# A graph attention layer on one core: x parts of more chunks ahead of the last stage, residuals further ahead, the shift split on ScalarE

## The chip, the core and the metric

The kernel runs on one core of a Trainium2 chip. The core has five engines, each with its own instruction queue: PE (TensorE, matrix products into PSUM), DVE (VectorE), ACT (ScalarE), POOL (GpSimd) and SP (SyncE, which here only issues DMAs). PSUM has eight banks of 128 partitions by 512 fp32 numbers. The metric is the device time of one execution in microseconds (us); lower is better.

## What is computed

12500 nodes with 128 features, 212500 edges sorted by target. In the reference, cut to what matters:

```python
Q, K, V = x @ WQ, x @ WK, x @ WV                    # 8 heads of 16
Eh = edge_attr @ WE
score = exp(clip(sum(K[src] * Q[dst] / 4 * Eh), -5, 5))
wV = segment_sum(V[src] * score, dst);  Z = segment_sum(score, dst)
h = x + wV / (Z + 1e-6)
h = (h - mean(h, nodes)) * rsqrt(var(h, nodes) + 1e-5) * bn_gamma + bn_beta
out = layernorm(x + h)                              # over the 128 features
```

The batch normalisation over nodes means that no output can be made before the last edge is done. With its factors a (scale) and b (offset) for each feature, the last stage computes layernorm(x + a*h + b) for each node.

## The kernel before, in words

Features lie on the 128 partitions: hx holds h transposed, 128 x 12500, and is updated in place. The edges are worked in groups g = 0 to NG-1 of up to eight tiles of 128 edges (L695 to L743). In each group POOL issues gathers of K and V rows, PE multiplies the edge features (`ehqe`, banks ps_e and ps_q), ACT and DVE form the products, PE turns them back (`turn_back`, L514, ps_t), DVE multiplies with K (`products`, L523), reduces to scores, ACT exponentiates, DVE forms the messages (L540), and PE sums them by target (`gather_sum`, L555 and L554, ps_a). ACT reads the sums out (L560), DVE divides (`denom`, `recip`, `attn`), PE turns the result and adds x (`add_x`, L580 and L581), ACT writes it into hx (`x_out`, L585), and DVE takes statistics (`bn_part`, L588). The order on each engine is written out by hand; each engine runs its list in that order and waits on semaphores.

After the groups come `norm_factors` (L357 to L362: the factors ab) and the last stage, `last_stage`, over 25 chunks of 512 nodes (the last has 212), taken in pairs: 0, 1, then (2,3), (4,5) to (22,23), and 24. For each chunk PE has to hold, in one bank, the centred sum x + a*h + b, nodes on partitions. `cent` is the matrix that subtracts the mean over features. There are two ways:

- A chunk in AHEAD: PE adds three products in the bank: the x part, `part_of_x` (L685, XR times cent, four matmuls), the h part (L820, hx times scaled_cent, four matmuls) and the shift b (L823 for chunk 0 in fp32, else L827, which multiplies bf16 pieces of the shift by ones). The x part doesn't need the factors, so `ahead(i)` can run it early, in the bank the chunk will use.
- Any other chunk: a residual y = a*h + x is made in SBUF, and PE centres it (L832, four matmuls). On POOL (odd chunks and 24) it takes two instructions (L799, L800) and includes b; on DVE (`on_vector`, even chunks from 8) one (L797), and PE adds the shift.

`split_shift` (L802 to L811) makes the shift: a small product into a bank, then five DVE instructions that split it into three bf16 rows. For each pair, ACT then squares one chunk whole (L847, DVE reduces it at L848) and the other in four pieces with accumulation (L852), takes the root (L854); DVE forms the reciprocal (L858) and the scaled output (L864), and SP stores it (L866). Banks are given out in the order of RING, chunk i taking entry i mod 8.

The order of the last stage is a software pipeline over the pairs:

```python
for i in range(len(pairs) + 4):
    for f, k in ((residual, i), (centred, i - 1), (variance, i - 1), (scaled, i - 2)):
```

so the residual of a pair stands one step ahead of its matmuls and squares. The residual buffers y are six. Before the change AHEAD is 0, 1, 2, 3, 4, 10 and 18; the x part of chunk 0 runs in the last group (L701), that of chunk 1 after add_x of the last group but one (L752), those of 2, 3 and 4 after the last add_x (L760), and those of 10 and 18 in the last stage itself.

Of the kernel before, what the change touches and what calls it, by code (L numbers as in the profile page):

```python
# [8 lines left out]
F32 = mybir.dt.float32  # L9
BF16 = mybir.dt.bfloat16  # L10
I32 = mybir.dt.int32
AF = mybir.ActivationFunctionType
# [4 lines left out]
P = 128  # L17
# [45 lines left out]
def gnn_kernel(  # L63
# [19 lines left out]
    nc = tc.nc  # L83
# [4 lines left out]
    NG = NW // 2  # L88
# [11 lines left out]
    psp = pps.enter_context(tc.tile_pool(name="psum", bufs=1, space=bass.MemoryType.PSUM))  # L100
# [105 lines left out]
    def issue(n=0):  # L206
        while len(queued) > n:
            f, *a = queued.pop(0)
            f(*a)

    def pace(step):
        if queued:
            f, *a = queued.pop(0)
            tc.add_manual_dep(f(*a).ins, step.ins.name,
                              mybir.DependencyInfo(mybir.DependencyClass.Sync, mybir.DependencyReason.DATA),
                              reason="pace")
# [13 lines left out]
    def fetch_rows(g, k, i):  # L230
        if i == 0:
            by_row[g] = rows.tile([P, 1, 2 * P], F32, name="byrow", bufs=2)
        _, ids = nc.values_load_multi_w_load_instructions(
            row_ids[i:i + 1, k * ROWS:(k + 1) * ROWS], engines=(ET.SP,), min_val=0, max_val=N - 1,
            skip_runtime_bounds_check_because="node ids")
        for p, r in enumerate(ids, i * ROWS):
            nc.sync.dma_start(by_row[g][p:p + 1, 0, :], kvd[ds(r, 1), :])
# [57 lines left out]
    def within(f, g):  # L295
        return f(g) if 0 <= g < NG else None
# [99 lines left out]
    B4 = 4 * P  # L396
# [4 lines left out]
    def width(i):  # L401
        return min(B4, N - i * B4)
# [172 lines left out]
    NEW = {}  # L575

    def add_x(g):
        NEW[g] = ps = (psp.tile([P, 4, P], F32, name="ps_e", bufs=2)[:, 0, :] if NG - 3 <= g < NG - 1 else
                       small_ps[:, 1, :])
        nc.tensor.matmul(ps, AT[g], ident, start=True, stop=False)  # L580
        return nc.tensor.matmul(ps, ident, XW[g], start=False, stop=True)  # L581
# [50 lines left out]
    for q in range(NQ):  # L632
# [3 lines left out]
        for g, a in piece.get(q, []):  # L636
            if a == 0:
                i = free.pop(0)
# [5 lines left out]
        k = q - first_step  # L644
# [28 lines left out]

    AHEAD = [0, 1, 2, 3, 4, 10, 18]
    RING = ["ps_q", "ps_q", "ps_t", "ps_t", "ps_e", "ps_e", "ps_a", "ps_m"]

    def blocks(i):
        n = width(i)  # L680
# [2 lines left out]
    def part_of_x(i, ps):  # L683
        for k, m in blocks(i):
            nc.tensor.matmul(ps[:m, k, :], XR[i][:, k * P:k * P + m], cent, start=(k == 0), stop=False)  # L685
# [3 lines left out]
    def ahead(i):  # L689
        if i in AHEAD:  # L690
            r = RING[i % len(RING)]
            PX[i] = psp.tile([P, 4, P], F32, name=r, bufs=RING.count(r))
            part_of_x(i, PX[i])

    for g in range(NG):  # L695
        within(load, g + 4)
        within(load_rel, g + 5)
        if g in fill:
            fetch_rows(*fill[g])
        within(products, g)  # L700
        if g == NG - 1:  # L701
            ahead(0)
        within(both_halves, g + 1)
        step = within(add_x, g - 3)
        step = within(q_mm, g + 3) or step
        if step is not None and queued:
            pace(step)
        issue()
        within(gather_sum, g - 1)
        if g + 1 < nxg and g + 1 not in SLOT:  # L710
            for _ in project_main(g + 1):
                pass
        within(turn_back, g + 1)
        within(scores, g)
        within(clip_exp, g)
        within(q_hi, g + 3)
        within(x_out, g - 3)
        within(sums_out, g - 1)
        within(q_lo, g + 2)
        within(denom, g - 2)  # L720
        within(recip, g - 2)
        within(attn, g - 2)
        within(q_window, g + 4)
        within(turned_onehot, g + 3)
        within(ehqe, g + 2)
        within(q_mid, g + 3)
        if g == NG - 1:
            add_x(g - 2)
        within(message, g)
        within(onehot, g + 1)  # L730
        if g == 2:
            load_last()
        for r in runs[1:]:
            if g == max(4, r[0] // 2 - 12):
                place(r)
        if g >= first_check and (g - first_check) % every == 0:
            check((g - first_check) // every)
        while free and todo and not pending:
            load_x()
        if g == NG - 2:  # L740
            flag = [nc.values_load(bad_i[0:1, 0:1], min_val=0, max_val=1 << 20,
                                   skip_runtime_bounds_check_because="a count")]
        bn_parts(2 * g - 5, 2 * g - 3)  # L743
# [5 lines left out]
    recip(last - 1)  # L749
    attn(last - 1)  # L750
    add_x(last - 1)
    ahead(1)  # L752
    sums_out(last)
    x_out(last - 1)
    denom(last)
# [1 line left out]
    attn(last)  # L757
    bn_parts(2 * last - 3, 2 * last + 1)
    add_x(last)
    for i in (2, 3, 4):  # L760
        ahead(i)
    x_out(last)
    for j in range(NCH):
# [6 lines left out]
    pairs = [[i] for i in range(min(2, NY))] + [list(range(i, min(i + 2, NY))) for i in range(2, NY - 1, 2)]  # L770
    if pairs[-1][-1] < NY - 1:
        pairs.append([NY - 1])
    if len(pairs[-1]) > 1 and width(NY - 1) < B4:
        pairs[-1:] = [[NY - 2], [NY - 1]]
    on_vector = {i for i in range(8, NY, 2) if width(i) == B4 and i not in AHEAD}
    by_reduce = {0, 2} | {i for i in range(3, NY, 2) if width(i) == B4}

    def last_stage(fin, bank, PX):
        Y, PY, V = {}, {}, {}
# [6 lines left out]
        shift = fin.tile([P, P], BF16, name="shift", bufs=1)  # L786
        scaled_cent = fin.tile([P, P], F32, name="scaled_cent", bufs=1)

        def residual(i):

            c, n = i * B4, width(i)
            if i in AHEAD:
                return
            Y[i] = fin.tile([P, B4], F32, name="y", bufs=6)
            y, h = Y[i][:, :n], hx[:, c:c + n]
            if i in on_vector:
                nc.vector.scalar_tensor_tensor(y, h, ab[:, 0:1], XR[i][:, :n], op0=OP.mult, op1=OP.add)  # L797
            else:
                nc.gpsimd.tensor_scalar(y, h, ab[:, 0:1], ab[:, 1:2], op0=OP.mult, op1=OP.add)  # L799
                nc.gpsimd.tensor_tensor(y, y, XR[i][:, :n], op=OP.add)  # L800

        def split_shift():  # L802
            ps = bank(6)[:65, 0, :]
            nc.tensor.matmul(ps, ab[:, 1:2].to_broadcast([P, 65]), cent, start=True, stop=True)
            rest = fin.tile([P, P], F32, name="rest", bufs=1)
            mid = fin.tile([P, P], BF16, name="mid", bufs=1)
            nc.vector.tensor_copy(shift[:65], ps)
            nc.vector.tensor_sub(rest[:65], ps, shift[:65])
            nc.vector.tensor_copy(mid[:65], rest[:65])
            nc.vector.tensor_copy(shift[32:33], mid[32:33])  # L810
            nc.vector.tensor_sub(shift[64:65], rest[64:65], mid[64:65])  # L811

        def centred(i):
            PY[i] = ps = PX[i] if i in PX else bank(i)
            c, full = i * B4, i in AHEAD
            if full:
                if i not in PX:
                    part_of_x(i, ps)
                for k, m in blocks(i):
                    nc.tensor.matmul(ps[:m, k, :], hx[:, c + k * P:c + k * P + m], scaled_cent, start=False,  # L820
                                     stop=False)
            if i == 0:
                nc.tensor.matmul(ps, ab[:, 1:2].to_broadcast([P, P]), cent[:, None, :].to_broadcast([P, 4, P]),  # L823
                                 start=False, stop=True)
                split_shift()
            elif full or i in on_vector:
                nc.tensor.matmul(ps, pick[:65], shift[:65, None, :].to_broadcast([65, 4, P]), start=not full,  # L827
                                 stop=full)
            if not full:
                whole = i in on_vector  # L830
                for k, m in blocks(i):
                    nc.tensor.matmul(ps[:m, k, :], Y[i][:, k * P:k * P + m], cent, start=not whole,  # L832
                                     stop=(k == 3 or not whole))
# [35 lines left out]
                    nc.sync.dma_start(out[c + k * P:c + k * P + m, :], o[:m, h, k, :])  # L869

        nc.vector.tensor_scalar(scaled_cent, cent, ab[:, 0:1], None, op0=OP.mult)
        for i in range(len(pairs) + 4):
            for f, k in ((residual, i), (centred, i - 1), (variance, i - 1), (scaled, i - 2)):
                if 0 <= k < len(pairs):
                    if f in (residual, centred):
                        for c in pairs[k]:
                            f(c)
                    else:
                        f(pairs[k])

    with tc.tile_pool(name="fin", bufs=3) as fin:
        last_stage(fin, lambda i: psp.tile([P, 4, P], F32, name=RING[i % 8], bufs=RING.count(RING[i % 8])), PX)
    pps.close()
# [140 lines left out]
```

## Time and profile before

| | |
|---|---|
| median of 3 runs | 2147.52 us (2146.24 to 2150.62) |
| the profiled execution | 2148.77 us, its span 2147.0 us |
| busy: PE, DVE, POOL, ACT | 1689.2, 1637.6, 1588.5, 626.3 us |
| last gathered sums of the last group (end of L555) | 2091.5 us |
| factors known (end of L362) | 2096.29 us |
| last DVE instruction ends | 2140.10 us |
| mean granted TensorE clock | 0.935 |

A busy PE includes waiting inside its pipeline, so its share isn't a distance from its peak. A timeline row gives start, duration, engine, line, operation, what is written and read with shapes, and in brackets the idle time before it and what ended it. An fp32 matmul shows as two rows of the PE count: "x8" is four matmuls. Line numbers are those of the kernel before; after the change lines from L702 on stand one to five lines lower.

### The profile page before, as it was taken

The numbers are of one execution on the slowest core, as the hardware profiler recorded it, in microseconds if no ns is written. First come the engines' busy times: TensorE is split into PE (matmuls) and PEld (weight loads), VectorE is DVE, ScalarE is ACT, GpSimd is POOL, SyncE is SP. The second block draws the span as 40 slices with busy tenths as digits, with TensorE's granted clock in tenths as the row PEclk, the third lists the DMA queues.
The fourth block names the chain that finished last, engine by engine and source line by source line (L and its number), as shares of the span: only waits on it lengthen the run. The fifth ranks groups of instructions, "written<-read, shape, count | busy, mean of one in ns | idle before, by whom it ended". The sixth has DMA issues, their size and how long they took to land. (4 is left out here: it accounts for less than half of the span.)

```text
span 2147.0 us, 36604 instructions
## 1 busy us (share of the span) xinstructions
PE 1689.2 (79%) x9398; PEld 1112.1 (52%) x9398; DVE 1637.6 (76%) x3574; ACT 626.3 (29%) x2472; POOL 1588.5 (74%) x1683
## 2 busy tenths in 40 slices
PE   8898888777777777777777877777777777777786
PEld 7565555444445454544555554545454445555455
DVE  4669999777877777777787777777777777777776
ACT  3343333232322222222222222222322222222225
POOL 7776777777777777777777777777777777777754
PEclk9999999999999999999999999999999999998988
DMA  9866666556555555555655555555655655655754
GB/s 302 277 189 183 180 201 190 176 169 178 170 179 168 173 173 167 178 172 167 180 167 175 174 170 177 167 179 157 182 180 168 180 168 155 193 168 155 228 169 122
DMA packets 179729, 386.77 MB, mean 180 GB/s; under 512 B 41838, under 2 KB 96151, under 8 KB 179511
## 3 DMA queue, kind: packets, MB, share of 16 engines
q0 software_dynamic: 78128, 212.05, 33.9%
q1 hardware_dynamic: 98038, 169.83, 25.6%
q10 hardware_dynamic: 3345, 2.48, 0.4%
q8 instruction: 77, 1.26, 0.2%
q14 instruction: 141, 1.16, 0.2%
HBM read 364.57 MB, written 19.63 MB: 179 GB/s over the span
## 5 line engine op out<-in xcount | busy, mean ns | idle before, releaser
L200 POOL DMA_INDIRECT slot<-kvd,srcs x1585 | 1502.2, 948 | 492.7 <-issue 430.6
L555 PE MATMUL ps_a<-msg,oh 128*128 128x136 f32 (+1 forms) x3322 | 573.9, 316 | 0.0
L523 DVE TENSOR_TENSOR p<-slot,ps_t 128x512 f32<-128x512 f32 (+1 forms) x408 | 272.0, 676 | 360.9 <-DMA slot<-kvd,srcs 336.2
L555 PEld LDWEIGHTS ps_a<-msg,oh 128*128 128x128 f32 (+1 forms) x3322 | 468.0, 185 | 86.4 <-issue 66.5
L535 ACT ACTIVATE ps_m<-s 128x64 f32<-128x64 f32 x208 | 47.3, 228 | 1328.0 <-DVE s L533 966.6
L493 PE MATMUL ps_e<-ea,w_e 128*128 128x512 f32 x832 | 409.0, 615 | 3.1 <-DMA ea<-eaT 2.8
L580 PE MATMUL ps_m<-ident,at 128*128 128x128 f32 x412 | 102.1, 332 | 304.6 <-DVE oh L457 299.5
L514 PE MATMUL ps_t<-ident,wt 128*128 128x128 f32 x1661 | 244.9, 286 | 104.7 <-DVE wt L506 103.5
L580 PEld LDWEIGHTS ps_m<-ident,at 128*128 128x128 f32 x412 | 66.2, 202 | 396.4 <-ACT q L483 353.5
L506 DVE TENSOR_TENSOR wt<-wt,ps_q 128x512 f32<-128x512 f32 x416 | 265.2, 678 | 1.8 <-PE ps_q L501 1.8
L514 PEld LDWEIGHTS ps_t<-ident,wt 128*128 128x128 f32 x1661 | 187.3, 144 | 144.3 <-DVE wt L506 140.6
L528 DVE TENSOR_REDUCE s<-p 128x64 f32<-128x1024 f32 x208 | 251.4, 1208 | 0.0
L540 DVE TENSOR_TENSOR msg<-slot,ps_m 128x1024 f32<-128x1024 f32 (+1 forms) x204 | 244.6, 1199 | 0.2
L495 ACT ACTIVATE wt<-ps_e 128x512 f32<-128x512 f32 x416 | 228.3, 584 | 23.0 <-PE ps_e L493 19.8
L493 PEld LDWEIGHTS ps_e<-ea,w_e 128*128 128x128 f32 x832 | 148.6, 199 | 110.5 <-issue 85.4
L501 PE MATMUL ps_q<-ot,q 64*128 64x512 bf16 x1248 | 171.2, 380 | 0.0
L454 DVE TENSOR_TENSOR oh<-ps_m,rel_i 128x512 f32<-128x512 f32 x208 | 141.6, 681 | 0.0
L501 PEld LDWEIGHTS <-q 64*128 64x128 bf16 x1248 | 44.1, 94 | 186.9 <-issue 162.1
L443 ACT ACTIVATE xw<-hx 128x64 f32 x416 | 84.1, 248 | 60.0 <-issue 51.5
L585 ACT ACTIVATE hx<-ps_m 128x64 f32 x412 | 90.3, 219 | 7.8 <-PE ps_m L581 1.0
L474 PE MATMUL ps_m<-w_q,xw 128*128 128x128 f32 x416 | 90.9, 304 | 1.3 <-ACT xw L443 0.9
L571 DVE SCALAR_TENSOR_TENSOR at<-os,keep,rz 128x128 f32<-128x128 f32 x208 | 73.2, 352 | 24.5 <-PE ps_e L493 0.9
(159 smaller groups left out, 1556.5 us busy)
## 6 DMA issues: line engine op xcount, KB each, us to landing
ea<-eaT SPq DMA_DIRECT2D x207, 512.0 KB
rb<-relT SPq DMA_DIRECT2D x414, 64.0 KB
slot<-kvd,srcs POOLq DMA_INDIRECT x1585
byrow<-kvd SPq DMA_DIRECT2D x1536, 1.0 KB
kvd<-t SPq DMA_DIRECT2D x24, 512.0 KB
slot<-xT SPq DMA_DIRECT2D x24, 256.0 KB
out<-o SPq DMA_DIRECT2D x24, 256.0 KB
hx<-xT SPq DMA_DIRECT2D x11, 512.0 KB
```

Source lines behind the costliest of these rows:

```text
L200: return nc.gpsimd.indirect_dma_start(out=out, out_offset=None, in_=table, in_offset=bass.IndirectOffsetOnAxis(ap=srcs[:, e:e + 1], axis=0))
L454: nc.vector.tensor_tensor(one, iota_ps[:, None, :].to_broadcast([P, n, P]), r[:, :n, None].to_broadcast([P, n, P]), op=OP.is_equal)
L493: nc.tensor.matmul(eh, w_e, EA[g][:, a:b, :].rearrange("p a b -> p (a b)"), start=True, stop=True)
L495: nc.scalar.activation(t[:, :(b - a) * P], eh, AF.Copy)
L501: nc.tensor.matmul(QE[g][h], Q3[g][r, k, :], OT[g][r, :(b - a) * P], start=(k == 0), stop=(k == 2))
L506: nc.vector.tensor_tensor(t, t, QE[g][h], op=OP.mult)
L514: nc.tensor.transpose(ps[:, j, :], WT[g][h][:, j * P:(j + 1) * P], ident)
L523: nc.vector.tensor_tensor(PR[g][:, c:d, :], KV[g](c, d, 0), PW[g][i][:, c - a:d - a, :], op=OP.mult)
L528: nc.vector.tensor_reduce(SS[g][:, :n, :], PR[g][:, :n, :].rearrange("p t (h d) -> p t h d", d=DH), axis=AX.X, op=OP.add)
L540: nc.vector.tensor_tensor(MSG[g][:, a:b, :P].rearrange("p t (h d) -> p t h d", d=DH), KV[g](a, b, P).rearrange("p t (h d) -> p t h d", d=D ...
L555: nc.tensor.matmul(AGG[g][WN if j >= n else 0:], OH[g][j], MSG[g][:, j, :], start=(j == 0), stop=(j == n - 1))
L580: nc.tensor.matmul(ps, AT[g], ident, start=True, stop=False)
```

## The change

```diff
     def add_x(g):
-        NEW[g] = ps = (psp.tile([P, 4, P], F32, name="ps_e", bufs=2)[:, 0, :] if NG - 3 <= g < NG - 1 else
+        NEW[g] = ps = (psp.tile([P, 4, P], F32, name="ps_t", bufs=2)[:, 0, :] if NG - 3 <= g < NG - 1 else
...
-    AHEAD = [0, 1, 2, 3, 4, 10, 18]
-    RING = ["ps_q", "ps_q", "ps_t", "ps_t", "ps_e", "ps_e", "ps_a", "ps_m"]
+    AHEAD = [0, 1, 2, 3, 4, 5, 6, 12, 18]
+    RING = ["ps_e", "ps_e", "ps_q", "ps_q", "ps_t", "ps_t", "ps_a", "ps_m"]
...
         if g == NG - 1:
-            ahead(0)
+            ahead(2)
+            ahead(3)
...
+        if g == NG - 2:
+            ahead(0)
+            ahead(1)
         within(turn_back, g + 1)
...
     add_x(last - 1)
-    ahead(1)
...
     add_x(last)
-    for i in (2, 3, 4):
+    for i in (4, 5, 6):
         ahead(i)
...
-            Y[i] = fin.tile([P, B4], F32, name="y", bufs=6)
+            Y[i] = fin.tile([P, B4], F32, name="y", bufs=8)
...
-            ps = bank(6)[:65, 0, :]
+            ps = bank(7)[:65, 0, :]
...
-            nc.vector.tensor_copy(shift[:65], ps)
+            nc.scalar.activation(shift[:65], ps, AF.Copy)
             nc.vector.tensor_sub(rest[:65], ps, shift[:65])
-            nc.vector.tensor_copy(mid[:65], rest[:65])
-            nc.vector.tensor_copy(shift[32:33], mid[32:33])
+            nc.scalar.activation(mid[:65], rest[:65], AF.Copy)
+            nc.scalar.activation(shift[32:33], mid[32:33], AF.Copy)
             nc.vector.tensor_sub(shift[64:65], rest[64:65], mid[64:65])
...
             c, full = i * B4, i in AHEAD
+            if i == 0:
+                split_shift()
             if full:
...
-            if i == 0:
+            if i < 2:
                 nc.tensor.matmul(ps, ab[:, 1:2].to_broadcast([P, P]), cent[:, None, :].to_broadcast([P, 4, P]),
                                  start=False, stop=True)
-                split_shift()
...
-        for i in range(len(pairs) + 4):
-            for f, k in ((residual, i), (centred, i - 1), (variance, i - 1), (scaled, i - 2)):
+        for i in range(len(pairs) + 5):
+            for f, k in ((residual, i), (centred, i - 2), (variance, i - 2), (scaled, i - 3)):
```

Chunks 5, 6 and 12 join AHEAD and chunk 10 leaves it. The x parts of chunks 0 and 1 now stand on PE in the last group but one, between its `gather_sum` and the last group's `turn_back`, in the ps_e banks; those of 2 and 3 after that `turn_back`, in ps_q; those of 4, 5 and 6 after the last `add_x`, in ps_t and ps_a; those of 12 and 18 in the last stage. The sums of add_x of the two groups before the last lie in ps_t in place of ps_e. Chunk 1 gets the fp32 shift like chunk 0. The small product of the shift now stands ahead of chunk 0 on PE, in the ps_m bank, and three of the five instructions that split it are on ACT. The residual of a pair stands two steps ahead of its matmuls, with eight buffers; chunks 8, 10, 14, 16, 20 and 22 have theirs on DVE (before: 8, 12, 14, 16, 20, 22), and POOL makes ten (before: twelve).

## The prediction

> **What bounds the kernel now.** I read the page first, then the busy time of each engine by stretch, the waits of the last 45 us, the timeline there, and the granted clock in stretches of 1 us.
>
> The page gives the span and, in 40 slices of 53.7 us, the TensorE clock.
>
> ```profile
> span 2147.0 us, 36604 instructions
> ...
> PEclk9999999999999999999999999999999999998988
> ```
>
> The change touches only the last 75 us, which are less than two of these slices; the two thousand microseconds before them are the same instructions in the same order. So the whole forecast is a matter of this tail. Its stretches, with busy time of PE, PE weight loads, DVE, ACT and POOL, then clock, DMA share and GB/s:
>
> ```profile
> 2074.75:2078.39 3.64, 0.00 (x0) 0.00 (x0) 1.20 (x3) 0.00 (x0) 2.73 (x4) 1.00 0.57 194
> 2078.39:2096.29 17.90, 15.88 (x91) 13.34 (x91) 11.68 (x33) 5.19 (x20) 1.53 (x5) 0.71 0.09 22
> 2096.29:2104.00 7.71, 5.41 (x34) 4.61 (x35) 4.33 (x10) 2.11 (x10) 7.16 (x8) 0.92 0.01 2
> 2104.00:2119.00 15.00, 13.28 (x90) 12.62 (x89) 9.82 (x19) 9.22 (x39) 7.71 (x8) 0.81 0.50 137
> 2119.00:2135.80 16.80, 13.65 (x109) 11.83 (x107) 14.90 (x29) 13.37 (x62) 9.36 (x10) 1.00 0.61 168
> 2096.29:2140.10 43.81, 32.34 (x228) 29.06 (x228) 33.14 (x67) 27.32 (x119) 24.22 (x24) 0.92 0.49 133
> ```
>
> 2096.29 is the end of L362, when the normalisation factors are known; 2140.10 is the end of the last DVE instruction. In between, the last stage takes 43.81 us, of which DVE works 33.14. The reader is to see that DVE is nearly full after 2119 (14.90 of 16.80) and far from it before: 3.38 idle, then 5.18. PE is idle for the whole of the first stretch (3.64 us), and after it runs at a mean clock of 0.71.
>
> The waits after 2096 name what DVE lacks:
>
> ```profile
> DVE v L848 <- ACT sq L847: 6.5, 7, 1.4
> ACT v L854 <- DVE v L848: 3.8, 2, 3.0
> DVE shift L807 <- PE ps_a L804: 2.5, 1, 2.5
> PE ps_q L827 <- DVE shift L811: 1.9, 1, 1.9
> ```
>
> DVE waits for squares (6.5 us), ACT for a reduction, PE for the shift. The timeline shows the shift as a chain on DVE that keeps the reduction of chunk 0 waiting, though its square ended at 2099.36:
>
> ```profile
> 2098.98 0.29 DVE L807 CAST shift<-ps_a 65x128 bf16<-65x128 f32 x1 [2.45 <-PE ps_a L804]
> 2099.63 1.18 DVE L809 CAST mid<-rest 65x128 bf16<-65x128 f32 x1
> 2101.03 0.60 DVE L811 TENSOR_TENSOR shift<-rest,mid 1x128 bf16<-1x128 f32 x1
> 2101.67 0.69 DVE L848 TENSOR_REDUCE v<-sq 128x4 f32<-128x512 f32 x1
> ```
>
> Last, the clock. PE idles from 2099.84 to 2101.69, and at 2102.9 the granted clock falls:
>
> ```profile
> 2100.00:2101.00 1.00, 0.00 (x0) 0.00 (x0) 0.97 (x2) 0.00 (x0) 1.00 (x2) 1.00 0.00 0
> 2103.00:2104.00 1.00, 1.00 (x5) 0.91 (x5) 0.62 (x1) 0.94 (x6) 0.92 (x2) 0.50 0.00 0
> ```
>
> It is 0.50 from 2102.9 to 2106.1, from 2113.0 to 2116.4 and from 2079.0 to 2089.1: always about 3.4 us or three times that, after a stretch in which PE was idle for 1.7 us or more.
>
> The Trainium skill ("TensorE: Matmul & The Clock Gate", Part 1) says that the clock is halved after an idle window of some 3.4 us and restored after a busy one. The 3.4 us agree; this trace halves the clock after a window that was idle for about 1.9 us only. By the page no cold window would be feared in the changed tail; by the rows one can come.
>
> **The change, part by part. 1. Chunks 0 and 1 ahead, before the last group's transposes.** Eight matmuls of L685 (x part, 128x128) enter PE between 2074.75 and 2078.39, where PE waits for DVE's L506, which itself waits for a gather. At full clock four cost 0.90 (2126.43 to 2127.33), eight 1.8: covered by the 3.64. At half clock four took 2.04, eight 4.1: then the transposes (L514), queued behind, come 0.45 late. The x chunks were issued at 2043.6, before the edge tile at 2045.45 that PE reads at 2068.4, so they are there; the ps_e banks were read out by ACT at 2070.03. Chunks 2 and 3 follow the transposes, eight matmuls where before there were four; PE next has to wait until 2083.2 for DVE's L457 anyway, and from 2079.23 even 4.1 us end at 2083.3. So 0 to +0.5, taken as 0.
>
> What it brings is the clock. gather_sum of the last group but one ran at 0.50 from 2084.21 to 2089.08 (4.87 us); the same fourteen rows, carry and closing pair one group earlier, at 1.00, took 2072.07 to 2074.75 (2.68). With PE busy in more of the stretch this run can be at full clock; then 2.2 us go, until the last messages (DVE L540, to 2087.13) and the read-out of the sums are late next: some 1.8 remain. PE still idles from about 2081 to 2083.2, and a window can hold that. Bounds 0 and 2.2; I take 1.3, nearer to the warm row. All behind it (sums, attention, statistics, factors) moves along.
>
> **2. add_x in ps_t, chunks 4 to 6 after it.** Two small products change their bank; ps_t is last read by L523, over at 2084.35, and needed at 2088: nothing. Chunks 4, 5, 6 replace 2, 3, 4 from 2093.35 to 2096.1, beside ACT and DVE working on the factors: nothing.
>
> **3. The shift on ScalarE, and first.** DVE loses L807, L809 and L810: 0.29 + 1.18 + 0.18 = 1.65. ACT gains three. An ACT row of 128x128 costs 0.26 to 0.28. The chain: the small product at about 2096.45, its result 2096.95, ACT 2097.25, DVE subtraction (0.29) 2097.65, ACT 2098.0, ACT 2098.3, DVE (0.18 to 0.60) 2098.6 to 2099.0. Before it was there at 2101.63; PE wants it at about 2101.3, so its wait of 1.9 goes. Behind these on ACT stands the square of chunk 0, which needs PE's chunk 0: that ended at 2098.72 and now has the small product ahead of it, 0.3: 2099.0. Hidden by 0.7; if a POOL instruction of 1.27 holds up each DVE step, the square is up to 1.2 later. Copy after Sqrt loads no table: L585 ran after the load at 2089.41 without another. Chunk 1 now has the fp32 shift (L823, about 0.9) in place of 0.22: +0.7 on PE.
>
> The Trainium skill ("SBUF — State Buffer", the shared port rule) says that a DVE copy or cast and a GpSimd instruction that meet exclude each other for the length of one. The 1.18 us cast fits it: it ended at 2100.81, the POOL addition beside it at 2100.72. By the page the last DVE subtraction can still be held; the rows above allow for that.
>
> **4. Residuals one pair further ahead.** Now y (L797) is made on DVE one pair before its matmuls, and PE, ACT and DVE form a loop: L797 at 2123.75, matmuls to 2126.60, square to 2127.24, reduction 2127.26 after 0.57 idle. With one more pair between, the 6.5 us of waits for squares have cover. The eight buffers keep POOL from waiting at the deeper lead; POOL has ten chunks in place of twelve, 2.1 each. On SP nothing changes place: the stores only come due earlier, and at 6.4 MB in some 34 us they need 190 GB/s, where the 1 us rows reach 291.
>
> **5. The sum.** Start to start without waits, DVE takes 2.76 for a pair with L797 (2120.99 to 2123.75), 2.08 without; ACT 2.29 (2118.27 to 2120.56). PE: a chunk of AHEAD with its x part there 1.11 (2127.33 to 2128.44), plain 0.89.
>
> DVE: the first reduction at 2099.65 (square 2099.05 + 0.6). From the first reduction to the second took 2101.67 to 2104.99 = 3.32 with nothing but ACT's chunk 1 between, so 2102.97; the third 0.6 later; then 0.6 + 0.9 for chunk 1's reciprocal and output, 0.68 for L797, and red(5) at 2105.75; a pair with L797, red(7) 2108.5. Eight pairs to red(23), four with and four without: 11.0 + 8.3 = 19.3, so 2127.8. From red(23) to the end before: 2135.77 to 2140.10 = 4.33, so **2132.1**. ACT: sq(5) 2104.9, nine pairs of 2.29, sq(23) 2125.5: below. PE from 2096.45: 0.3 + 2 x 1.8 + 5 x 1.11 + 0.89 + six pairs with L797 of 2.0 + two pairs with x part of 2.9 + 0.45 = 28.6, so 2125.0: below by little. Gain 8.0. From it I take 0.9 for small waits, half of the 1.9 that DVE still idles between 2119.00 and 2135.80. Stage 7.1, front 1.3: 8.4.
>
> The profiled execution took 2148.77 in all, 1.8 around its span of 2147.0; the median of the runs is 2147.52. 2148.77 - 8.4 = 2140.4, and from the median 2139.1. I take **2139.5**.
>
> **The rivals.** (a) PE becomes the bound, and cold windows come back. For: PE has 28.6 us of work against DVE's 31.5, so each cold window of 3.4 us takes 1.7 of it and the slack is used up by the first. Against: with banks and shift there, PE never idles 1.7 us after 2083. With no front gain and such windows taking about 2.0: 7.1 - 2.0 = 5.1, 2142.4 from the median and 2143.7 from the profile, so some 2143. (b) The deeper lead gives nothing, since DVE was full after 2119; only the shift chain goes, 2101.67 to 2099.65 = 2.0: 2145.5. Against it speak the 5.18 idle before 2119. (c) Slower: the whole last stage at half clock. Then PE needs 57.2, and 4.6 from its last matmul to the end (2135.5 to 2140.1): 2158.1, 18 later than before, less 0 to 2 in front: about 2165. It decides from the number of cold windows: 28.6 + 1.7 n + 4.6 exceeds 43.8 at n over 6. In the trace the clock is back at 1 after each window with PE busy throughout (2089.1, 2106.1, 2116.4), so this is unlikely. That the change doesn't do what it says is excluded by the order of the instructions, which is as described.
>
> **How the numbers follow.** Forecast 66%, (a) 22%, (b) 8%, (c) 4%. What a measurement of this kernel can tell is 0.2%, 4.3 us: below 2143.2 is faster. The forecast lies there, and half of (a): 77%; the other half and (b) are the same, 19%; slower 4%. Range: below, the full stage gain of 8.0 and 2.2 in front from the median, 2137.3, and half of a lost cold window in the groups, 2136.5; above, no front gain and two cold windows, 2148.77 - 7.1 + 3.4 = 2145.
>
> **What would show it.** In the profile after: PE busy between 2074 and 2078; the run of L555 after it at a clock near 1 and under 3 us long; L831 not waiting for shift; the first reduction 3.3 to 3.7 us after the factors, not 5.4; reductions 2.1 and 2.8 us apart from there, and hardly a wait for squares; from the factors to the last output 36 to 37 us. I am wrong if the clock is at 0.50 in the last stage, if DVE waits for PE there, or if the stage is over 40 us.

## The result, and the profile after

The median is 2137.93 us (2136.77 to 2142.12, 8 runs) against 2145.85 us (2142.93 to 2150.62, 8 runs) for the kernel before beside it. The ratio is 0.9968, with a 95% interval of 0.9958 to 0.9977. On the median of before that is 6.9 us less, 4.9 to 9.0. The profiled execution took 2140.7 us, its span 2138.9 us, 8.1 less than the span of before.

The page of the kernel after, its span and the clock in 40 slices:

```profile
span 2138.9 us, 36636 instructions
...
PEclk9999999999899999999999999999999999999998
```

Then the busy times by stretch of the kernel after (start and end, length, busy time of PE, PE weight loads, DVE, ACT and POOL with instructions, granted clock, DMA share, GB/s). The factors are known at 2095.53 and DVE's last instruction ends at 2131.85:

```profile
2075.79:2078.65 2.86, 1.78 (x17) 1.59 (x15) 1.21 (x3) 0.00 (x0) 2.19 (x3) 1.00 0.63 225
2078.65:2095.53 16.88, 13.90 (x91) 11.79 (x91) 11.70 (x33) 5.19 (x20) 1.74 (x5) 0.90 0.10 23
2095.53:2103.20 7.67, 7.53 (x53) 6.44 (x54) 4.11 (x8) 4.52 (x16) 7.12 (x8) 1.00 0.13 37
2103.20:2118.20 15.00, 14.46 (x123) 13.84 (x122) 14.43 (x28) 12.58 (x58) 13.88 (x13) 1.00 0.58 160
2095.53:2131.85 36.32, 29.22 (x231) 26.81 (x231) 31.44 (x63) 27.40 (x122) 21.00 (x20) 0.95 0.58 159
```

The first row was a stretch without any PE work; now PE is busy for 1.78 of it. The last stage (the last row) takes 36.32 where it took 43.81, with DVE busy for 31.44 of it where it was 33.14. Between 2103 and 2118 DVE works 14.43 of 15.00; before, the stretch that answers to it held 9.82. The clock is 1.00 as long as PE has work in the stage (its last matmul ends at 2125.8; the 0.95 is the mean with the idle end).

The waits of the kernel after, from the factors to the end (engine, tile and line that waited, what ended it, us in total, times, longest):

```profile
ACT v L858 <- DVE v L852: 3.4, 5, 1.0
DVE v L852 <- ACT sq L851: 2.1, 2, 1.5
...
ACT shift L810 <- PE ps_m L807: 1.4, 1, 1.4
```

The waits for squares fell from 6.5 us in seven to 2.1 in two, both by 2102.1. DVE's wait of 2.5 and PE's of 1.9 around the shift are gone; what DVE waits for ACT within the shift is 0.65 and 0.38. The shift in the timeline of the kernel after:

```profile
2096.11 0.27 ACT L810 ACTIVATE shift<-ps_m 65x128 bf16<-65x128 f32 x1 [1.37 <-PE ps_m L807]
2096.42 0.29 DVE L811 TENSOR_TENSOR rest<-ps_m,shift 65x128 f32<-65x128 f32 x1 [0.65 <-ACT shift L810]
2096.74 0.31 ACT L812 ACTIVATE mid<-rest 65x128 bf16<-65x128 f32 x1 [0.35 <-DVE rest L811]
...
2097.08 0.93 DVE L814 TENSOR_TENSOR shift<-rest,mid 1x128 bf16<-1x128 f32 x1 [0.38 <-ACT mid L812]
...
2098.57 0.69 DVE L852 TENSOR_REDUCE v<-sq 128x4 f32<-128x512 f32 x1 [0.56 <-ACT sq L851]
```

The shift is complete at 2098.0, and the first reduction starts 3.04 after the factors, not 5.38. It waits for the square, no longer for the shift.

The 8.1 us of the span divide as follows, from the ends of instructions: the start of the last group's L506 comes 0.26 later (2077.79 to 2078.05), from there to the factors 1.02 less (18.50 to 17.48), the stage 7.49 less (43.81 to 36.32), from DVE's last instruction to the end of the span 0.15 more (6.90 to 7.05).

### The profile page after: what moved, and what is told of

It is laid out like the page before. It is cut to its first block, busy times and chain, and to the rows that moved or that the text cites. A ratio compares the mean times of both kernels' runs of the same rounds, so it can differ in the third digit from the quotient of the medians.

```text
span 2138.9 us, 36636 instructions
## 1 busy us (share of the span) xinstructions
PE 1679.5 (79%) x9417; PEld 1099.1 (51%) x9417; DVE 1637.6 (77%) x3571; ACT 626.4 (29%) x2475; POOL 1584.9 (74%) x1679
## 3 DMA queue, kind: packets, MB, share of 16 engines
q8 instruction: 77, 1.26, 0.2%
q14 instruction: 141, 1.16, 0.2%
## 5 line engine op out<-in xcount | busy, mean ns | idle before, releaser
L555 PE MATMUL ps_a<-msg,oh 128*128 128x136 f32 (+1 forms) x3322 | 563.2, 312 | 0.0
L555 PEld LDWEIGHTS ps_a<-msg,oh 128*128 128x128 f32 (+1 forms) x3322 | 457.0, 181 | 85.0 <-issue 63.6
L493 PE MATMUL ps_e<-ea,w_e 128*128 128x512 f32 x832 | 415.0, 624 | 2.4 <-DMA ea<-eaT 2.1
L580 PE MATMUL ps_m<-ident,at 128*128 128x128 f32 x412 | 99.5, 325 | 295.9 <-DVE oh L457 289.8
L506 DVE TENSOR_TENSOR wt<-wt,ps_q 128x512 f32<-128x512 f32 x416 | 265.5, 680 | 1.8 <-PE ps_q L501 1.8
L580 PEld LDWEIGHTS ps_m<-ident,at 128*128 128x128 f32 x412 | 64.8, 198 | 388.0 <-ACT q L483 322.8
L540 DVE TENSOR_TENSOR msg<-slot,ps_m 128x1024 f32<-128x1024 f32 (+1 forms) x204 | 244.8, 1200 | 0.2
```

Of the source, the lines that this page charges most:

```text
L493: nc.tensor.matmul(eh, w_e, EA[g][:, a:b, :].rearrange("p a b -> p (a b)"), start=True, stop=True)
L506: nc.vector.tensor_tensor(t, t, QE[g][h], op=OP.mult)
L540: nc.vector.tensor_tensor(MSG[g][:, a:b, :P].rearrange("p t (h d) -> p t h d", d=DH), KV[g](a, b, P).rearrange("p t (h d) -> p t h d", d=D ...
L555: nc.tensor.matmul(AGG[g][WN if j >= n else 0:], OH[g][j], MSG[g][:, j, :], start=(j == 0), stop=(j == n - 1))
```

## The experiments

**Theory:** the stage is now held by DVE alone, at what the walk along its queue gives; it needs all three parts, since each removes a wait that would otherwise stand in the place of the others. **Rival 1, the clock:** before lost the time to its two cold windows (stretches with the granted clock at 0.50), and the change helps because it leaves no hole in PE's work; shift and lead matter little. **Rival 2, the front:** the gain comes from the x parts in the gaps before the factors. The profiled executions, in us; "front" is from the start of the last group's L506 to the factors, "first reduction" is counted from the factors, "waits" are DVE's waits for squares in the stage:

| kernel | front | first reduction | stage | waits | cold windows while PE works in the stage |
|---|---|---|---|---|---|
| before | 18.50 | 5.38 | 43.81 | 6.5 | two |
| after | 17.48 | 3.04 | 36.32 | 2.1 | none |
| shift only | 18.50 | 3.15 | 39.27 | 4.5 | none |
| lead only | 17.36 | 5.38 | 39.35 | 1.4 | none |
| x parts moved back | 17.97 | 4.33 | 39.34 | 2.6 | none |
| after, gap filled | 16.33 | 3.21 | 36.83 | 2.2 | none |
| before, holes filled | 16.32 | 5.57 | 41.06 | 3.3 | none |
| two more residuals on POOL | 16.54 | 3.04 | 36.22 | 2.1 | none |
| lead undone | 16.54 | 3.03 | 40.55 | 4.6 | none |
| shift undone | 16.54 | 5.38 | 38.59 | 1.4 | none |
| gap filled, 16 and 22 ahead | 16.31 | 3.04 | 36.30 | 2.4 | none |
| before again | 16.32 | 5.38 | 42.18 | 5.1 | one |
| after again | 17.34 | 3.04 | 36.17 | 2.1 | none |

Four of these (before with holes filled, two more on POOL, lead undone, shift undone) ran on a chip where every kernel takes some 2640 us, since its groups take 500 us more; there the ratios are to before on the same chip, and the instructions of the last stage have the same durations. The kernel after was not timed on that chip, and each kernel has one profiled execution here (before and after have two), so a stage of the table is that of one execution.

**Shift only.** On the kernel before, the split of the shift as after the change, nothing else:

```diff
-            nc.vector.tensor_copy(shift[:65], ps)
+            nc.scalar.activation(shift[:65], ps, AF.Copy)
...
+            if i == 0:
+                split_shift()
...
-            if i == 0:
+            if i < 2:
```

> The kernel before with one part of the change: the shift first on PE, three of its five splitting steps on ACT, chunk 1 with the fp32 shift. Theory (the shift chain on DVE costs 2.0 us, and by PE's hole of 1.85 us also a cold window of the clock): the first reduction 3.1 to 3.6 us after the factors are known instead of 5.4, PE not waiting for the shift; last stage (factors known to last DVE instruction) 39 to 42 us instead of 43.8, depending on whether a cold window is left; whole -2 to -4 us. Rival (the shift hides beside other work): first reduction earlier, stage 43 or more, whole within 1 us of before.

Measured: 2142.30 against 2144.72 us, ratio 0.9991 (0.9981 to 1.0001). The first reduction comes at 3.15 as after the change, but 4.5 us of waits for squares stay, and the stage takes 39.27:

```profile
DVE v L849 <- ACT sq L848: 4.5, 6, 1.5
```

**Lead only.** On the kernel before, eight buffers and one pair more between residual and matmuls:

```diff
-            Y[i] = fin.tile([P, B4], F32, name="y", bufs=6)
+            Y[i] = fin.tile([P, B4], F32, name="y", bufs=8)
...
-        for i in range(len(pairs) + 4):
-            for f, k in ((residual, i), (centred, i - 1), (variance, i - 1), (scaled, i - 2)):
+        for i in range(len(pairs) + 5):
+            for f, k in ((residual, i), (centred, i - 2), (variance, i - 2), (scaled, i - 3)):
```

> The kernel before with one part of the change: residuals two pairs ahead, eight buffers; AHEAD, banks and shift as before. Theory (squares come late because a residual, its matmuls and its square follow each other): DVE's waits for squares fall from 6.5 us to about 3, those of PE for y vanish; the first reduction still 5.4 us after the factors; stage 39.5 to 42 us, whole -2 to -4 us. Rival (DVE was the bound from 2119 on, the deeper lead is of no use): stage 43 or more, whole within 1 us of before.

Measured: 2142.59 us, ratio 0.9992 (0.9982 to 1.0003). One wait for squares is left (1.4 us), the first reduction still stands at 5.38, the stage takes 39.35:

```profile
DVE v L848 <- ACT sq L847: 1.4, 1, 1.4
```

Two of DVE's six residuals (L797) were long in this stage, 1.18 and 1.78 where the others took 0.74; each ran beside a POOL instruction. Neither part alone can be told from no change by its time, and both intervals lie above that of the whole change.

**X parts moved back.** On the kernel after, chunk 0 in the last group and chunk 1 after the `add_x` of the last but one, as before the change; `AHEAD` is kept, so five x parts now stand after the last `add_x`:

```diff
         if g == NG - 1:
-            ahead(2)
-            ahead(3)
+            ahead(0)
...
-        if g == NG - 2:
-            ahead(0)
-            ahead(1)
...
+    ahead(1)
...
-    for i in (4, 5, 6):
+    for i in (2, 3, 4, 5, 6):
```

> The changed kernel with its x parts moved back: chunk 0 after the transposes of the last group, chunk 1 after the last add_x but one, chunks 2 to 6 after the last add_x. Theory (the early x parts keep PE's clock up in the last groups, and save PE time behind the last add_x): the run of L555 of the last group but one takes 4.5 to 4.9 us instead of 4.0, factors known about 1.0 us later counted from the last products that waited for a gather; five x parts (4.9 us) no longer fit beside the factors (2.9 us), so the first square is 1.5 to 2 us later and the stage 37.5 to 38.5 us instead of 36.3; whole +2 to +3 us against the changed kernel. Rival (the gaps were of no use): whole within 0.7 us of the changed kernel.

Measured: 2143.65 us, ratio 0.9998 (0.9987 to 1.0009): the whole gain is gone, where 2 to 3 us were expected to go. That is more than the front: the stage itself takes 39.34. Its timeline shows two reasons. The first is on PE (the factors are known at 2094.96):

```profile
2093.81 1.95 PE L685 MATMUL ps_t<-cent,slot 128*128 128x128 f32 x16
...
2095.59 1.06 PE L685 MATMUL ps_a<-cent,slot 128*128 128x128 f32 x8
...
2096.49 0.38 PE L804 MATMUL ps_m<-cent,ab 128*65 128x128 f32 x2
```

The last x part stands between the factors and the small product of the shift, so that everything behind comes 1.3 late (first reduction at 4.33, not 3.04). The second is on DVE:

```profile
2104.90 1.37 DVE L797 SCALAR_TENSOR_TENSOR y<-hx,ab,slot 128x512 f32<-128x512 f32 x1
...
2108.28 1.06 DVE L797 SCALAR_TENSOR_TENSOR y<-hx,ab,slot 128x512 f32<-128x512 f32 x1
...
2113.43 1.81 DVE L797 SCALAR_TENSOR_TENSOR y<-hx,ab,slot 128x512 f32<-128x512 f32 x1
```

Three of DVE's six residuals took 0.63, 0.32 and 1.07 longer than the 0.74 of the others: 2.0, where the kernel after has one such row with 0.46. The start 1.3, the rows 2.0 - 0.5 and 0.3 more of waits for the last stores are 3.1, for a difference of 3.0. Beside the 1.81 a POOL addition ran from 2113.42 to 2114.68; more on that below. So the gaps take in x parts that would otherwise stand on the path, but half of what the stage lost is a meeting of DVE and POOL. It depends on when the two start, and whether the x parts bring it each time isn't shown by one execution. By the ratios some 6 us are lost against the kernel after, give or take 3; the profiled executions show 3.5 of them (0.5 in front, 3.0 in the stage), and where the rest goes stays open.

**After, gap filled.** On the kernel after, eight more matmuls on the bank of chunk 3 ahead of its x part, which overwrites their result, to close the hole in which PE idles before L580:

```diff
+            if i == 3:
+                fill_in(i, PX[i])
+                fill_in(i, PX[i])
```

> The changed kernel with the x part of chunk 3 computed three times, the first two results overwritten: eight more matmuls, 1.8 us at full clock, in the hole of 1.95 us that PE still has behind the x parts of the last group. Theory (the clock fell at 2083.5 because the window before held this hole): no fall there, the run of L555 behind it 2.7 to 3.0 us instead of 4.0, factors 0.7 to 1.0 us earlier; stage unchanged at 36.3; whole -0.7 to -1.0 us. Rival (the clock falls for another reason, or the sums are not what the factors wait for): L555 still 4 us, or factors no earlier; whole 0 to +0.3 us.

The hole and its price in the kernel after, as the timeline has it:

```profile
2083.49 0.76 PE L580 MATMUL ps_m<-ident,at 128*128 128x128 f32 x2 [1.95 <-DVE oh L457]
...
2084.47 3.09 PE L555 MATMUL ps_a<-msg,oh 128*128 128x136 f32 x14
```

With the hole filled:

```profile
2083.04 1.93 PE L555 MATMUL ps_a<-msg,oh 128*128 128x136 f32 x14
...
2086.48 1.31 PE L555 MATMUL ps_a<-msg,oh 128*128 128x136 f32 x8 [0.31 <-DVE msg L540]
```

Measured: 2138.36 us, ratio 0.9974 (0.9964 to 0.9984). The front falls to 16.33 (16.31 in the other kernel with this gap filled, below; 17.48 and 17.34 in the two executions with the hole), and the next wait is for the messages (L540), as the prediction's part 1 had it. In the whole time nothing can be told from the kernel after: the intervals overlap, and the stage of this execution was 0.5 longer, with two of DVE's residuals at 1.15 and 1.16 where the kernel after has one at 1.20.

**Before, holes filled.** On the kernel before, matmuls in the stage's two holes, on banks that are written anew later:

```diff
+                if i in (1, 8):
+                    spare = bank(7) if i == 1 else ps
+                    fill_in(i, spare)
+                    fill_in(i, spare)
```

> The kernel before with two of PE's holes in the last stage filled: eight matmuls more behind chunk 1's h part (into a spare bank) and eight more at the head of chunk 8 (into its own bank, overwritten). Nothing else changes. Theory (of the 43.8 us of the profiled stage some 3 were two cold windows of the clock, which PE's holes of 1.85 and 1.72 us brought): no clock at 0.50 between the factors and the end, stage 40 to 41.5 us; whole 0 to -2 us, since not each execution of before has both cold windows. Rival (DVE or ACT bound there, the clock of no account): stage 43 to 44 us, whole within 0.5 us.

Measured: ratio 0.9987 (0.9973 to 1.0001). The stage of the kernel before with no cold window, in the columns of the stretches above:

```profile
2592.01:2633.07 41.06, 32.87 (x260) 29.46 (x260) 33.42 (x67) 27.38 (x119) 24.64 (x24) 0.99 0.50 137
```

So by these two executions the two cold windows made 2.75 of the 43.81, and the parts of the change have 41.06 - 36.32 = 4.74 to explain without them. (The added matmuls cost something themselves: the first reduction comes at 5.57, 0.2 later than before.) Rival 1 is right about a third of the profiled gain and wrong about the rest. Against 41.06 the shift alone gave 1.8 and the lead alone 1.7.

**Two more residuals on POOL.** On the kernel after, chunks 16 and 22 on POOL in place of DVE, to see whether DVE's work sets the stage:

```diff
-    on_vector = {i for i in range(8, NY, 2) if width(i) == B4 and i not in AHEAD}
+    on_vector = {i for i in range(8, NY, 2) if width(i) == B4 and i not in AHEAD + [16, 22]}
```

> The changed kernel with the residuals of chunks 16 and 22 made on POOL in place of DVE (POOL 12 chunks, DVE 4). Theory (DVE bounds the stage from the first reductions on, POOL has slack: it ended at 2118 of 2132): DVE loses 2 x 0.68 = 1.4 us, PE two shifts of 0.22; stage 36.3 to 35.0 or 35.2, POOL last at about 2121; whole -0.8 to -1.2 us, if the stores, which ran at 288 GB/s in the last 4 us, don't take it back. Rival 1 (the stores bound the end): stage shorter, tail from the last DVE instruction to the end longer by as much, whole within 0.3 us. Rival 2 (POOL comes late): PE waits for y, stage 36.5 or more.

Measured: ratio 0.9977 (0.9961 to 0.9993), stage 36.22 where 35.0 to 35.2 was expected: a miss. Two rows of 0.74 went from DVE, but others grew:

```profile
2615.39 1.26 POOL L803 TENSOR_TENSOR y<-y,slot 128x512 f32<-128x512 f32 x1
2615.40 1.80 DVE L800 SCALAR_TENSOR_TENSOR y<-hx,ab,slot 128x512 f32<-128x512 f32 x1
...
2632.88 0.69 DVE L868 TENSOR_TENSOR o<-ps_a,v 128x512 f32<-128x512 f32 x1 [0.36 <-DMA out<-o]
```

DVE's residual that started with POOL's addition took 1.80 in place of 0.74 (another took 1.20, as in the kernel after), and at the end DVE waited for an output buffer that a store still held. The sum fits the walk along DVE's queue: 1.48 us of work went, the residuals left took 1.07 more beyond their 0.74 than in the kernel after, and the waits for stores were 0.2 longer. That leaves some 0.2, and the stage was 0.1 shorter. So DVE had hardly less to do, and this run can't show by its length whether DVE alone holds the stage.

**Lead undone** and **shift undone**, each on the kernel after:

```diff
-            Y[i] = fin.tile([P, B4], F32, name="y", bufs=8)
+            Y[i] = fin.tile([P, B4], F32, name="y", bufs=6)
...
-            for f, k in ((residual, i), (centred, i - 2), (variance, i - 2), (scaled, i - 3)):
+            for f, k in ((residual, i), (centred, i - 1), (variance, i - 1), (scaled, i - 2)):
```

> The changed kernel with the residuals back to one pair ahead of their matmuls and six buffers. Theory (the lead covers the squares): DVE waits for squares again, 4 to 6 us in place of 2.1; stage 38.0 to 39.0 us in place of 36.3; whole +1.7 to +2.7 us against the changed kernel. Rival (with the shift off DVE and PE fed early the lead is no longer needed): stage 36.5 or less, whole within 0.5 us of the changed kernel.

```diff
-            nc.scalar.activation(shift[:65], ps, AF.Copy)
+            nc.vector.tensor_copy(shift[:65], ps)
...
-            if i == 0:
-                split_shift()
...
+                split_shift()
```

> The changed kernel with the shift as before: after chunk 0 on PE, its five splitting steps on DVE, chunk 1 with the bf16 shift. Theory (the chain on DVE holds the first reduction, 5.4 us after the factors in place of 3.0, and DVE is the bound behind it): stage 38.0 to 38.7 us in place of 36.3, up to 1.7 more where PE's hole in front of the shift brings a cold window; whole +1.7 to +2.4 us against the changed kernel. Rival (the lead makes up for a late start): stage under 37 us, whole within 0.5 us of the changed kernel.

Measured: without the lead 0.9998 (0.9985 to 1.0011), stage 40.55, 4.2 over the change and above the 38.0 to 39.0 expected; without the shift's move 0.9986 (0.9969 to 1.0004), stage 38.59, 2.3 over it, as expected. The waits without the lead:

```profile
POOL y L802 <- PE ps_e L836: 6.6, 2, 4.8
DVE v L852 <- ACT sq L851: 4.6, 6, 1.5
...
PE ps_e L836 <- DVE y L800: 3.1, 2, 1.7
```

The loop that the prediction described is back, with every engine in it: PE waits for DVE's residual, DVE for ACT's square, and POOL, with only six buffers, for PE. The clock was at 1 as long as PE had work, so rival 1 can't explain the 4.2. Nor can rival 2: both kernels keep the x parts in front, and both have a front of 16.54.

Here the theory has to give way in one point. By the stages as they stand, each part is worth more on top of the others (lead 4.2, shift 2.3) than alone (1.7 and 1.8), as it said. But DVE's residuals were longer by 1.4 without the lead (1.23 and 1.63), by 1.5 with the lead only, by 0.5 in the kernel after and by 0.3 in before with its holes filled. Taken off, the lead is worth 1.7 + 1.5 - 0.3 = 2.9 alone and 4.2 - 1.4 + 0.5 = 3.3 on top, the shift 1.8 and 2.3 (its pairs differ by 0.1 at most in these rows). 2.9 and 1.8 are 4.7, and the whole is 4.9 (41.06 - 36.32 = 4.74, and 0.2 for the longer residuals, 0.5 in the one and 0.3 in the other). So the two nearly add up. That neither helps without the other isn't shown. The x parts without the other two were not run.

**Gap filled, 16 and 22 ahead.** The filled gap, and chunks 16 and 22 in `AHEAD`, so that DVE loses two residuals and PE gains two x parts:

```diff
-    AHEAD = [0, 1, 2, 3, 4, 5, 6, 12, 18]
+    AHEAD = [0, 1, 2, 3, 4, 5, 6, 12, 16, 18, 22]
```

> The changed kernel with the hole of the last group filled as in e4_gap_filled (repeated x part of chunk 3) and chunks 16 and 22 in AHEAD, their x parts made by PE in the last stage in place of the residual on DVE. Theory (two more on POOL brought nothing, because DVE's remaining L800 were blocked by POOL's additions, 1.80 and 1.20 us in place of 0.74; on PE there is no such block): DVE loses 2 x 0.68, PE gains 2 x 0.9 and ends near 2 us later than in the changed kernel, still ahead of DVE's last 5 us; stage 35.3 to 36.0 us in place of 36.3, factors as early as with the hole filled (16.3 to 16.5 us after the last group's L506 in place of 17.0); whole -0.7 to -1.5 us against the changed kernel. Rival (PE becomes the bound): stage 36.5 or more, PE without idle time up to its end.

Measured: 2141.81 against 2150.05 us, ratio 0.9962 (0.9948 to 0.9976), stage 36.30: it missed as well. It is the lowest ratio of the study, but its interval contains that of the kernel after nearly whole, so it is not shown to be faster. Its stretch from 2118 to 2128 and one later reduction:

```profile
2118.00:2128.00 10.00, 10.00 (x89) 9.84 (x88) 9.55 (x21) 9.29 (x43) 0.56 (x1) 1.00 0.88 241
```

```profile
2113.53 1.81 DVE L807 SCALAR_TENSOR_TENSOR y<-hx,ab,slot 128x512 f32<-128x512 f32 x1
...
2128.81 0.69 DVE L859 TENSOR_REDUCE v<-sq 128x4 f32<-128x512 f32 x1 [0.32 <-ACT sq L858]
```

PE is busy for 10.00 of 10.00, and DVE waits for a square again at the end: with two x parts more PE has no slack left. One residual met POOL's addition and took 1.81, another a POOL scaling and took 1.19, so that most of the two residuals' 1.48 was lost again: what was taken from DVE's queue came back as waits and longer rows.

**Both kernels again,** unchanged, for one more profile of each.

> The kernel before, a second profiled execution. Theory (the clock's windows run free of the kernel, so the cold windows fall differently each time): from the last group's L506 to the factors between 16.3 us (none cold) and 18.5 us, stage between 41.1 (none cold) and 43.8 us. Rival (the cold windows belong to the program): both within 0.2 us of the first profile, 18.5 and 43.8.

> The changed kernel, a second profiled execution. Theory: stage 36.2 to 36.6 us whatever the windows, since PE has no hole of 1.7 us in it; to the factors 16.3 to 17.5 us, as the hole behind the x parts of the last group falls into one window or not. Rival: a cold window in the stage, 38 us or more.

Measured: spans of 2143.7 and 2141.3 us. The stage of before took 42.18, with one cold window in place of two, and its front 16.32, with the run of L555 at full clock (1.93); that of after took 36.17, and its front 17.34. The spans differ by 2.4 only: in the execution of after the last group's L506 came 3.1 later (2080.87 for 2077.75), and the front took 1.0 more. So before's tail is different from one execution to the next, and after's stage was not in these two.

## Why the prediction was right, step by step

The prediction was 2139.5 us, with a range of 2136.5 to 2145; the median of 2137.93 lies in it. The forecast was 1.6 too high, about as much as its starting point: the median of before, 2147.52 in three runs, came out at 2145.85 in eight. The gain in its sum was 8.4; by the ratio it was 6.9, between the medians 7.9. That it came so near is in part luck: 1.3 of the 8.4 stood for the front, which the two pairs of profiles show 1.0 shorter and 1.0 longer, and 2.75 of the stage's difference hang on cold windows that another execution has only in part.

**What bounds the kernel.** Right: the end was set by waits around DVE in the last stage. What the reading left out is that one execution was taken for the kernel. 43.81 contained 2.75 of cold windows that another execution has in part (42.18), so a stage gain computed as a difference to 43.81 is that of a poor execution. The gain in the median, 6.9, lies between the 4.74 without windows and the 7.49 of the two profiles.

**1. X parts ahead of the last group's transposes.** Free in this execution, as said: PE was busy for 1.78 us in a stretch in which it idled (estimate 1.8), and the wait before the transposes still ended with L506. On the chip with the longer groups they were not free: there PE had no wait before the transposes, and the front was 16.54 in three kernels with these x parts, 16.32 in before with its holes filled, with the clock at 1.00 in all four. The benefit is the step that was mis-sized. Taken were 1.3 between bounds of 0 and 2.2; this pair of profiles shows 1.02. But the run of L555 did not come near full clock: with its carry and its last pair, as the prediction counted its 4.87, it took 3.84 us (2084.47 to 2088.31), where under 3 was the mark. The remaining hole, feared from 2081 to 2083.2, was 1.95 us long, and the clock fell behind it. In the kernel after:

```profile
2082.00:2083.00 1.00, 0.00 (x0) 0.00 (x0) 0.96 (x3) 0.00 (x0) 0.00 (x0) 1.00 0.00 0
...
2084.00:2085.00 1.00, 1.00 (x7) 1.00 (x6) 0.97 (x3) 0.00 (x0) 0.00 (x0) 0.50 0.01 4
```

And as before's own front is 18.50 in one execution and 16.32 in another (18.50 and 17.36 with the shift only and the lead only, which leave it as it was), the 1.02 is no gain of the change that two profiles could show: where the windows fall decides. The larger worth of the gaps was not in the sum: they take chunks 2 and 3 off the stretch just before the factors. With five x parts there the first reduction comes 1.3 later, though AHEAD has the same nine chunks.

**2. The small products in ps_t and chunks 4 to 6 after them.** Nothing, as said. The last x part ended at 2095.43, 0.1 before the factors, so there was no room for one more; this is what the version with the x parts moved back ran into.

**3. The shift.** Right in place and size. The shift was there at 2098.0 (2098.6 to 2099.0 expected, from factors 0.76 later: 2.5 after them where 2.3 to 2.7 was said). The first reduction came at 3.04 for 3.36, and L831 never waited for the shift. The last subtraction was held as feared: 0.93 us for one row. It cost nothing, because DVE still had to wait 0.56 for the square. Alone the step is worth 1.8, in the company of the others 2.3; the 2.0 of rival (b) lies between.

**4. The lead.** Right, and the largest part: 4.2 of the stage by the profiles, some 3 without the meetings of DVE and POOL. The 6.5 us of waits shrank to 2.1. Rival (b), that a deeper lead has no use, falls with that.

**5. The sum.** The walk along DVE's queue was the step that carried the forecast. It gave a stage of 35.8 without and 36.7 with the allowance of 0.9; it took 36.32 and 36.17. Reductions stand 2.76 and 2.08 apart as taken:

```profile
2104.84 0.67 DVE L852 TENSOR_REDUCE v<-sq 128x4 f32<-128x512 f32 x1
...
2107.60 0.68 DVE L852 TENSOR_REDUCE v<-sq 128x4 f32<-128x512 f32 x1
...
2109.68 0.67 DVE L852 TENSOR_REDUCE v<-sq 128x4 f32<-128x512 f32 x1
```

What stood in the allowance was not known when it was taken: 0.46 for a residual beside a POOL instruction, and 0.15 for a store that had to release its buffer. PE's work was below DVE's by little: 29.2 busy for 28.6, over 30.3 after the factors (2125.8) where the sum had 28.7.

**The rivals.** (a) did not come in this kernel, with no window between the factors and PE's last matmul in two executions; its first half, PE without slack, comes when PE gets two more x parts. (c) had nothing for it.

What stays open: how often before's tail falls into one, two or more cold windows. Two executions don't tell, so the median gain of 6.9 can't be divided exactly between removed waits and removed windows. Where the rest of the loss with the x parts moved back lies is open too. The new places in RING were not tried alone, since the banks are tied to the x parts.

## What to carry to other kernels

Where three engines hand work around a loop, walk the busiest engine's queue with all the waits gone, and trust that sum if the other engines' own sums stay below it: it held within 0.5 us here. Put work that doesn't depend on a late result into gaps before it, but count what still stands between that result and its first use. And before a gain is computed from one profile, or two parts are compared by one profile each, ask which rows another execution might not have: here 2.75 of 43.81 us came and went with the clock, and up to 1.5 with the meetings of two engines.

## What the runs showed of the hardware

**Residuals on DVE and POOL instructions exclude each other.** DVE's residual (two inputs from SBUF, 128x512) takes 0.74 alone. Started within 0.1 us of a POOL addition (1.26 to 1.27) it took 1.78 to 1.81, in four kernels; started some 0.1 us after a POOL scaling of 0.77 to 0.78 had begun, 1.18 to 1.20 (lead only, after). In all these it ended 0.53 to 0.56 after POOL's row. In the kernel after POOL's next addition took 1.58 in place of 1.27:

```profile
2114.40 0.78 POOL L802 TENSOR_SCALAR y<-hx,ab 128x512 f32<-128x512 f32 x1
...
2114.51 1.20 DVE L800 SCALAR_TENSOR_TENSOR y<-hx,ab,slot 128x512 f32<-128x512 f32 x1
...
2115.26 1.58 POOL L803 TENSOR_TENSOR y<-y,slot 128x512 f32<-128x512 f32 x1
```

The Trainium skill ("SBUF — State Buffer", Who interferes with whom) says that a DVE instruction with two SBUF inputs and a GpSimd instruction that reads SBUF exclude each other for a whole instruction. These rows agree, and such rows took back 1.07 of the 1.48 us when two residuals were moved from DVE to POOL.

**The clock can fall after less than 2 us of idle PE, and need not.** 1.95 us without PE work, in the profile after, were followed by some 3.4 us at 0.50 (2083.5 to 2086.9), as 1.85 were in that of before, and 1.95 again in the second profile of after. But 1.85 us with the lead only and with the shift undone, and 2.45 in the second profile of after (2073.10 to 2075.55), had no such stretch behind them.

**A copy on ScalarE next to POOL keeps its time.** The cast of 65x128 took 1.18 on DVE beside a POOL addition in the kernel before, and 0.31 on ACT, at 2096.74 beside one from 2096.60 to 2097.87, in the kernel after. DVE's subtraction of a single row, started beside the same addition, took 0.93.

**Near the end the stores keep the DMA engines busy throughout.** In the kernel after the output DMAs move this much, between the last reductions and the end:

```profile
2128.70:2132.80 4.10, 0.00 (x0) 0.00 (x0) 2.85 (x9) 1.14 (x6) 0.00 (x0) 0.50 1.05 288
```

288 GB/s, with a DMA share of 1.05, while DVE waited 0.15 for an output buffer; in the version with two more residuals on POOL it waited 0.36.
